# A two-layer network with routed experts in one launch: a run of one-hot products a row in the first layer's front, eight buffers for the experts' results, and the next layer's weights loaded at other places

## The chip, the core and the metric

The kernel runs on one core of one Trainium2 chip. Everything is fp32, but for the small masks and one-hots in bf16. The metric is the device time of one execution in microseconds. What can be told from no change for this kernel is about 0.5%.

A core has five engines that run side by side and meet at semaphores: TensorE (matmuls and transposes into PSUM), VectorE, ScalarE, GpSimd, and SyncE (SP), which issues most of the transfers. In the profile they are PE (PEld is its weight load), DVE, ACT, POOL and SP. Each works through its own queue in order.

## What is computed

Two layers follow each other on `x` of 4 rows x 512 tokens x 256 channels. Each normalizes, scales and shifts by a modulation, attends, adds back through a gate, and does the same around a feed-forward part.

```python
# layer 0: linear attention over each row, then routed experts
h = layernorm(x) * (1 + ca) + sa
q, k, v = split(h @ W + b)
x = x + ga * (q / |q|) * sum(k / |k| * v)          # norms and sum over the 512 tokens of a row
h = layernorm(x) * (1 + cb) + sb
logits = h @ gate_w.T                               # 32 experts in 8 groups; 3 groups kept
topk_w, topk_idx = top_k(softmax(masked), 6)
pos = cumsum(one_hot(topk_idx)) - 1                 # place of a token in its expert, over all rows
slot = expert * 48 + pos if pos < 48 else none      # 48 places an expert
y = (silu(g) * u) @ w_down[e]                       # g, u = split(x_of_slot @ w_gate_up[e])
x = x + gb * (sum_k 16 * topk_w * y[slot] + shared_expert(h))
# layer 1: 16-head causal attention, then a gated feed-forward with spline weights
```

## The kernel before

The first layer has two stages. The **front** goes through the four rows `b` one after the other (the loop `for b in range(B)` that the diff changes), and interleaves by hand, on TensorE, the pieces of several rows. The pieces are Python generators; `some(parts, n)` takes the next `n` steps of one. TensorE's instructions stay in the order in which they are written (`manual_schedule`). The other engines' queues are put in order at build by a planner, from estimated times and from the order of writing; `issue_after(ins)` keeps a block's instructions behind `ins` on the engine of `ins`. The pieces are:

- `linear_attention(b, half)`: three projections `p` (L352) of 128 channels, for values, keys and queries. ScalarE writes `vT`, squares the keys with a sum (L370), writes `qT` (L376) and squares it with a sum (L378). VectorE forms the sum over keys and values (L372). GpSimd raises the two sums to the power -1/2 (`n`, L379). VectorE then scales `kv` (L381) and forms `o` (L383).
- `attention_output(b)`: transposes `at_a` of `o` (L253), the addition to `x` (L257), the statistics, the power `rs_m` on GpSimd (L201), and the normalized `xn_m` (L213, L217).
- `attention_input(b)` and `moe_input(b)`: transposes `lt_a`, `lt_m` (L235) and the modulated copies `hT_a`, `hT_m` (L237).
- `table_rows(b)`: eight GpSimd products and sums on `xn_m` (L576, L577), and the store of the row's tokens to a table in DRAM. The gather of the experts reads this table.
- `logits(b)` and `choose(b)`: the products `plg` (L589), the transposed `plv` (L600), and on VectorE the choice of groups and experts, up to the mask `selb` (L654) and the weights `wr` (L655), with one exponential on ScalarE (L635).
- `place(b)`: the running count `pos` by matmuls (L663 to L674) and its copy `posb` (L683). For row 0 GpSimd ranks each token's experts in the steps `rk` (L688 to L696). Then, four times a row, a one-hot `oh` (128 x 1536, bf16, two buffers) on VectorE (L706) and four matmuls `pix` (L710) that turn it into slot indices, summed in `ixs` (L719).
- `shared(b)`: six products a row for the shared expert (`sg`, `su`, L736), 24 in all, taken as filler through `sh`; ScalarE and VectorE take them to `sT` (L744, L746).

In row `b`'s pass, the placing of row `b - 1` runs among the logits and the choice of row `b`: each of the four one-hots is followed by its matmuls and then by another piece. After the loop the matmuls `pid` (L805) bring the slot indices into columns, and the GpSimd gathers `xg` of the tokens (L887) start from them.

The **expert stage** goes through 16 pairs of experts. The weights `wg`, `wd` lie in eight slots: six are loaded during the front, two when the front's memory is free, and pair `q + 8` when pair `q` has freed its slot. A pair is gathered (`xg`), turned (`xt`), multiplied (`gu`, L906), turned again (`act_t`) and multiplied down (`y`, L929; one PSUM buffer). ScalarE evicts `y` to `ysb` (L943; four buffers). SP writes `ysb` to the DRAM array `ytab` (L974). For the first twelve pairs GpSimd scatters it to `planes` (L959), from which row 0's sums are read back as `yr` (L1013) when all scatters have landed. The last four pairs (`direct`) go to row 0 by a one-hot product instead (`pc`, L988); their one-hot lies in the slot of a `wd` that is no longer needed, their `ysb` in four buffers of its own (tag `ysd`). VectorE and GpSimd sum `yr` (L1029 to L1033), the row is normalized for layer 1, and layer 1's first projections `pj` start.

The loads of layer 1's first weights (`load_qk`, L846; `load_v`, L855) are written after pair 7, kept behind the last expert load.

Of the kernel before, what the change touches and what calls it, by code (L numbers as in the profile page):

```python
# [18 lines left out]
P = 128  # L19
# [17 lines left out]
SHARES = (0, 0, 0)  # L37
LAST = 1
# [47 lines left out]
def kernel(ctx: ExitStack, tc: tile.TileContext, a: dict, out: bass.AP):  # L86
# [225 lines left out]
    with ExitStack() as l0:  # L312
# [31 lines left out]
        def linear_attention(b, half, sp, ps):  # L344
# [24 lines left out]
            junk = sp.tile([P, T], F32, tag="junk", name=f"j{b}{half}", bufs=1)  # L369
            nc.scalar.activation(junk, pk, AF.Square, bias=bk, accum_out=n2[:, 0:1])  # L370
            junk2 = sp.tile([P, T], F32, tag="junk2", name=f"jj{b}{half}", bufs=1)
            nc.vector.scalar_tensor_tensor(junk2, pk, bk, vT, ALU.add, ALU.mult, accum_out=kv)  # L372
            yield
            pq = project(half)
            qT = sp.tile([P, T], F32, tag="qT", name=f"qT{b}{half}")
            nc.scalar.activation(qT, pq, AF.Identity, bias=bq[:, half : half + 1])  # L376
            junk = sp.tile([P, T], F32, tag="junk", name=f"j2{b}{half}", bufs=1)
            nc.scalar.activation(junk, qT, AF.Square, accum_out=n2[:, 1:2])  # L378
# [3 lines left out]
            o = sp.tile([P, T], F32, tag=f"o{half}", name=f"o{b}{half}", bufs=1)  # L382
# [220 lines left out]
        def choose(b, lg):  # L603
# [9 lines left out]
            gr = rp.tile([P, NTT, 16], F32, tag="gr", name=f"gr{b}")  # L613
# [28 lines left out]
            sel = rp.tile([P, NTT, E], F32, tag="sel", name=f"sel{b}")  # L642
# [15 lines left out]
        def place(b):  # L658
# [25 lines left out]
            if b:  # L684

                nc.gpsimd.memset(wr[:, :, 1, :], float(1 << 20))
            else:

                rk = [fc.tile([P, NTT, E], F32, tag=f"rk{u}", name=f"rk{u}") for u in range(2)]
                nc.gpsimd.tensor_copy(rk[0][:, :, 1:], selb[:, :, 0 : E - 1])  # L690
                nc.gpsimd.memset(rk[0][:, :, 0:1], 0.0)
                for u, w in enumerate((1, 2, 4, 8, 16)):
                    src, dst = rk[u % 2], rk[(u + 1) % 2]
                    nc.gpsimd.tensor_copy(dst[:, :, 0:w], src[:, :, 0:w])
                    nc.gpsimd.tensor_tensor(dst[:, :, w:], src[:, :, w:], src[:, :, 0 : E - w], ALU.add)
                nc.gpsimd.tensor_tensor(wr[:, :, 1, :], rk[1], six.to_broadcast([P, NTT, E]), ALU.add)  # L696
# [5 lines left out]

            pix = psa.tile([P, CAP, 8], F32, tag="lgix", name=f"pix{b}", bufs=1)
            for i in range(NTT):
                oh = rp.tile([P, CAP, E], BF16, tag="oh", name=f"oh{b}{i}", bufs=2)
                nc.vector.tensor_tensor(  # L706
                    oh, posb[:, i : i + 1, :].to_broadcast([P, CAP, E]), iota_c, ALU.is_equal
                )
                for q in range(4):
# [3 lines left out]
                        rhs=oh[:, :, 8 * q : 8 * q + 8],  # L713
# [3 lines left out]
                if i < NTT - 1:  # L717
                    yield
# [3 lines left out]
        shared_banks, last_silu = [False], [None]  # L722
# [28 lines left out]
        with tc.manual_schedule(engines={mybir.EngineType.PE}):  # L751
# [9 lines left out]
            for b in range(B):  # L761
# [4 lines left out]
                attention_output(b, sp, ps)  # L766
                some(part, 2 if more else 3)
                if more:
                    some(linear_attention(b + 1, 1, sp, ps), 4)
# [5 lines left out]
                some(placed)  # L775
# [5 lines left out]
                some(placed)  # L781
                some(sh)
                table_rows(b)
                pick = choose(b, next(lg))
                next(pick)
                some(placed)
                if not more or 0 < SHARES[b]:
                    some(sh)
                next(pick, None)
                for i in range(1, 3):  # L790
                    some(placed)
                    if not more or i < SHARES[b]:
                        some(sh)
                placed = place(b)
            some(sh, LAST)
            for n in (1, 1, 0, 0, 0):
                some(placed)
                some(sh, n)
# [4 lines left out]
        for m in range(4):  # L803
# [8 lines left out]
        with tc.manual_schedule(engines={mybir.EngineType.PE}):  # L812
            for _ in sh:
                pass
# [1104 lines left out]
```

## Time and profile before

| | us |
|---|---|
| three executions | 1154.89, 1148.79, 1153.67 |
| their median | 1153.67 |
| the profiled execution | 1150.32 |
| its span | 1148.6 |
| TensorE busy in the span | 1113.2 (97%) |
| VectorE busy | 849.7 (74%) |
| GpSimd busy | 625.5 (54%) |
| ScalarE busy | 544.1 (47%) |
| mean transfer rate over the span | 75 GB/s |

The profile is of one execution. Busy shares are averages over stages that differ: the front ends with `pid` at 131.5 us, the expert stage with layer 1's first projections at 227 us, and layer 1 takes the rest. In a timeline a row gives start, length, engine, line, operation, tile written and tiles read, and in brackets the idle time of the engine before it and what ended that. A clock of 1.0 is TensorE's full rate.

### The profile page before, as it was taken

What the parts mean: (1) busy time and instruction counts of PE and PEld (TensorE: products, weight loads), DVE (VectorE), ACT (ScalarE), POOL (GpSimd) and SP (SyncE); (2) the same over time, 40 slices, a digit from 0 to 9 for tenths busy, and PEclk for the clock granted to TensorE, in tenths of its full rate; (3) what the DMA queues carried; (4) which work ended last, traced back from release to release, by engine and by line L of the source; (5) the groups of instructions that cost most, each with busy time, mean ns of one, the idle gap of its engine ahead of it and who ended that gap; (6) DMA issues with size and microseconds to landing.
All of it is one profiled execution on the core that took longest, in us unless ns stands there. A gap on an engine that the chain in (4) does not pass through costs nothing.

```text
span 1148.6 us, 16948 instructions
## 1 busy us (share of the span) xinstructions
PE 1113.2 (97%) x5256; PEld 818.4 (71%) x5256; DVE 849.7 (74%) x2562; ACT 544.1 (47%) x1386; POOL 625.5 (54%) x944
## 2 busy tenths in 40 slices
PE   7988999999999999999999999999999999999998
PEld 3434454677777777777777777777777777888887
DVE  5669544677888878888788877988777776566765
ACT  4654233355545555555555555555555555333321
POOL 4445334368865768855756865435445655344331
PEclk9989999999999999999999999999999999999999
DMA  7830399735313223410421522111010000000000
GB/s 254 278 96 28 107 302 279 246 71 97 65 38 77 48 69 59 94 46 19 95 50 37 103 43 68 37 50 39 22 44 19 28 11 1 1 1 19 19 5 33
DMA packets 80486, 86.10 MB, mean 75 GB/s; under 512 B 12158, under 2 KB 64748, under 8 KB 80268
## 3 DMA queue, kind: packets, MB, share of 16 engines
q1 hardware_dynamic: 67868, 70.19, 19.6%
q0 software_dynamic: 11712, 13.25, 7.2%
q10 hardware_dynamic: 816, 1.58, 0.4%
q8 instruction: 42, 0.69, 0.3%
q14 instruction: 48, 0.39, 0.1%
HBM read 73.84 MB, written 11.55 MB: 74 GB/s over the span
## 4 chain that ended last, share of the span: by engine, by line
PE 74%; DVE 9%; ACT 3%; DMA 2%; issue 2%; POOL 1%; ACTq 0%; POOLq 0%; DVEq 0%; SPq 0%
PE s L1410 11%; PE o L1451 10%; PE po L1147 8%; PE P0p L1147 7%; PE fP L1147 6%; PE pt L1442 6%; PE P1p L1147 4%; PE P2p L1147 4%; PE P0v L1147 3%; PE acc L1147 3%; PE P2v L1147 2%; PE P1v L1147 2%; PE pd L823 2%; PE gu L906 1%; PE y L929 1%
## 5 line engine op out<-in xcount | busy, mean ns | idle before, releaser
L1425 ACT ACTIVATE p<-s,nm 128x512 f32<-128x512 f32 (+3 forms) x256 | 135.4, 529 | 119.9 <-DVE nm L1422 119.1
L1410 PE MATMUL s<-qk,qk 128*128 128x512 f32 (+3 forms) x512 | 170.4, 435 | 1.5 <-DVE qk L1318 1.4
L1451 PE MATMUL o<-pT,v 128*128 128x512 f32 (+3 forms) x512 | 148.5, 433 | 0.0
L1451 PEld LDWEIGHTS o<-pT,v 128*128 128x128 f32 x512 | 96.7, 190 | 54.7 <-issue 30.6
L1444 ACT COPY pT<-pt 128x512 f32<-128x512 f32 (+1 forms) x192 | 98.4, 513 | 67.1 <-PE pt L1442 66.9
L1422 DVE TENSOR_REDUCE nm<-s 128x1 f32<-128x512 f32 (+3 forms) x256 | 124.3, 485 | 4.0
L290 POOL DMA_INDIRECT ysum<-ytab,code x72 | 112.9, 1568 | 20.4 <-issue 14.8
L1427 DVE TENSOR_SCALAR p<-p,den 128x512 f32<-128x512 f32 (+3 forms) x256 | 118.1, 461 | 3.4
L1442 PEld LDWEIGHTS pt<-ident,p 128*128 128x128 f32 x640 | 81.6, 141 | 34.5 <-issue 10.5
L1442 PE MATMUL pt<-ident,p 128*128 128x128 f32 x640 | 101.7, 273 | 0.4 <-DVE p L1427 0.4
L1420 DVE TENSOR_TENSOR s<-s,mask 128x128 f32<-128x128 f32 x256 | 73.7, 288 | 30.1 <-PE s L1410 30.0
L1285 POOL TENSOR_TENSOR w_p<-w_q,w_k 128x128 f32<-128x128 f32 x63 | 39.2, 622 | 82.4 <-ACT t1p L1324 55.0
L1410 PEld LDWEIGHTS s<-qk,qk 128*128 128x128 f32 x512 | 77.4, 191 | 6.5 <-issue 1.9
L1147 PE MATMUL P0p<-hT_a,w_q 128*128 128x256 f32 x252 | 75.0, 379 | 0.0
L1293 POOL TENSOR_TENSOR w_p<-w_k 128x128 f32<-128x128 f32 x63 | 29.9, 474 | 80.4 <-PE P2p L1147 80.4
L1147 PEld LDWEIGHTS P0p<-hT_a,w_q 128*128 128x128 f32 x252 | 47.5, 190 | 33.1 <-issue 30.1
L1426 DVE RECIPROCAL den<-den 128x1 f32<-128x1 f32 x256 | 40.5, 158 | 37.9 <-ACT p L1425 35.4
L1147 PE MATMUL P1p<-fT,w_p 128*128 128x256 f32 x252 | 64.9, 380 | 1.1 <-DVE x L257 1.1
L1462 ACT ACTIVATE oH<-o,bia 128x512 f32<-128x512 f32 x64 | 43.9, 686 | 42.4 <-PE o L1451 41.6
L1155 POOL TENSOR_TENSOR fI<-it 128x256 f32<-128x256 f32 x30 | 21.8, 726 | 67.1 <-DVE it L1744 67.1
L1318 DVE SCALAR_TENSOR_TENSOR qk<-P0p,bia,u3p 128x256 f32<-128x256 f32 x63 | 30.4, 483 | 36.7 <-ACT qk L1339 36.0
L1147 PEld LDWEIGHTS P1p<-fT,w_p 128*128 128x128 f32 x252 | 47.6, 190 | 8.4 <-issue 2.1
(336 smaller groups left out, 2666.1 us busy)
## 6 DMA issues: line engine op xcount, KB each, us to landing
wg<-in_w_gate_up SPq DMA_DIRECT2D x16, 704.0 KB
w_q<-in_w_q SPq DMA_DIRECT2D x64, 128.0 KB
w_k<-in_w_k SPq DMA_DIRECT2D x64, 128.0 KB
w_v<-in_w_v SPq DMA_DIRECT2D x16, 512.0 KB
wd<-in_w_down SPq DMA_DIRECT2D x16, 352.0 KB
basis<-in_basis SPq DMA_DIRECT2D x8, 640.0 KB
planes<-zero SPq DMA_DIRECT2D x4, 768.0 KB
yr<-planes SPq DMA_DIRECT2D x4, 768.0 KB
```

The costliest lines, as they stand in the source:

```text
L290: ga = nc.gpsimd.indirect_dma_start(out=ysum[b][:, i, :], out_offset=None, in_=ytab[:, :], in_offset=bass.IndirectOffsetOnAxis(ap=code[:, ...
L1147: nc.tensor.matmul(out, lhsT=lhsT, rhs=rhs, start=start, stop=stop, skip_group_check=shared)
L1410: nc.tensor.matmul(s[:, at[i] : c], lhsT=qk[n, 0][:, i * P : (i + 1) * P], rhs=qk[n, 1][:, : (i + 1) * P], start=True, stop=True,)
L1420: nc.vector.tensor_tensor(s[:, e - P : e], s[:, e - P : e], mask, ALU.add)
L1422: nc.vector.tensor_reduce(nm, s[:, e - w : e], AX.X, ALU.max, negate=True)
L1425: nc.scalar.activation(p, s[:, e - w : e], AF.Exp, bias=nm, accum_out=den)
L1426: nc.vector.reciprocal(den, den)
L1427: nc.vector.tensor_scalar_mul(p, p, den)
L1442: nc.tensor.transpose(pt[:, c : c + P], probs[n, i][:, j * P : (j + 1) * P], ident)
L1444: nc.scalar.copy(pT, pt[:, :w])
L1451: nc.tensor.matmul(o[:, j * P :], lhsT=vs[n // 4][:, j, hc : hc + HD], rhs=pTs[n, j], start=(j == 0), stop=(j == NTT - 1),)
L1462: nc.scalar.activation(oT, o, AF.Identity, bias=bia[:, 2, h : h + 1])
```

## The change

Four things change.

1. In the front, the four one-hots of a row are made in one run, in four buffers instead of two, and the sixteen `pix` matmuls follow in one run later. The last step of the second half of `linear_attention` (`kv`, `o`) is written behind the one-hots and kept there with `issue_after(last_oh)`. The rank steps `rk` of row 0 are kept behind the last power written on GpSimd.
2. The table products of row `b - 1` are written into the pass of row `b`, behind `attention_output(b)`. The fillers of the shared expert are dealt out anew: 2, 4, 4 and 11 products in the four passes (2, 3, 3 and 10 before), two more behind the loop (3 before, with `LAST`), and one behind `pid` (3 before). `pid` is now in the written order on TensorE.
3. `ysb` has eight buffers. The `ysb` of the last four pairs lies with their one-hot in the freed `wd` slot. Memory for the new buffers comes from `junk` and `junk2`, whose results go to `qT`, `vT` and `o`, and from `gr` and `sel`, which get one buffer.
4. `load_qk(0)`, `load_v(0)` and `load_qk(1)` are written in the passes of pairs 9, 10 and 11, without the tie to the last expert load, and `load_qk(2)` behind the read-back.

```diff
             bk = bq[:, 2 + half : 3 + half]
-            junk = sp.tile([P, T], F32, tag="junk", name=f"j{b}{half}", bufs=1)
-            nc.scalar.activation(junk, pk, AF.Square, bias=bk, accum_out=n2[:, 0:1])
-            junk2 = sp.tile([P, T], F32, tag="junk2", name=f"jj{b}{half}", bufs=1)
-            nc.vector.scalar_tensor_tensor(junk2, pk, bk, vT, ALU.add, ALU.mult, accum_out=kv)
+
+            qT = sp.tile([P, T], F32, tag="qT", name=f"qT{b}{half}")
+            nc.scalar.activation(qT, pk, AF.Square, bias=bk, accum_out=n2[:, 0:1])
+            nc.vector.scalar_tensor_tensor(vT, pk, bk, vT, ALU.add, ALU.mult, accum_out=kv)
             yield
             pq = project(half)
-            qT = sp.tile([P, T], F32, tag="qT", name=f"qT{b}{half}")
             nc.scalar.activation(qT, pq, AF.Identity, bias=bq[:, half : half + 1])
-            junk = sp.tile([P, T], F32, tag="junk", name=f"j2{b}{half}", bufs=1)
-            nc.scalar.activation(junk, qT, AF.Square, accum_out=n2[:, 1:2])
+            o = sp.tile([P, T], F32, tag=f"o{half}", name=f"o{b}{half}", bufs=1)
+            nc.scalar.activation(o, qT, AF.Square, accum_out=n2[:, 1:2])
             last_pow[0] = nc.gpsimd.tensor_tensor(n2, n2, nhalf[:, 0:2], ALU.pow)
...
                 rk = [fc.tile([P, NTT, E], F32, tag=f"rk{u}", name=f"rk{u}") for u in range(2)]
-                nc.gpsimd.tensor_copy(rk[0][:, :, 1:], selb[:, :, 0 : E - 1])
...
+                with tc.issue_after(last_pow[0].ins):
+                    nc.gpsimd.tensor_copy(rk[0][:, :, 1:], selb[:, :, 0 : E - 1])
...
+            ohs = []
+            for i in range(NTT):
+                oh = rp.tile([P, CAP, E], BF16, tag="oh", name=f"oh{b}{i}", bufs=NTT)
+                last_oh[0] = nc.vector.tensor_tensor(
+                    oh, posb[:, i : i + 1, :].to_broadcast([P, CAP, E]), iota_c, ALU.is_equal
+                )
+                ohs.append(oh)
+            yield
             pix = psa.tile([P, CAP, 8], F32, tag="lgix", name=f"pix{b}", bufs=1)
             for i in range(NTT):
-                oh = rp.tile([P, CAP, E], BF16, tag="oh", name=f"oh{b}{i}", bufs=2)
-                nc.vector.tensor_tensor(
-                    oh, posb[:, i : i + 1, :].to_broadcast([P, CAP, E]), iota_c, ALU.is_equal
-                )
                 for q in range(4):
                     nc.tensor.matmul(
                         pix[32 * q : 32 * q + 32, :, :],
                         lhsT=tok[:, b * NTT + i, :],
-                        rhs=oh[:, :, 8 * q : 8 * q + 8],
+                        rhs=ohs[i][:, :, 8 * q : 8 * q + 8],
                         start=(i == 0),
                         stop=(i == NTT - 1),
                     )
-                if i < NTT - 1:
-                    yield
...
                 attention_output(b, sp, ps)
+                if b:
+                    table_rows(b - 1)
                 some(part, 2 if more else 3)
                 if more:
-                    some(linear_attention(b + 1, 1, sp, ps), 4)
+                    part = linear_attention(b + 1, 1, sp, ps)
+                    some(part, 3)
...
                 moe_input(b, sp, ps)
-                some(placed)
+                some(placed, 2)
+                if more:
+                    with tc.issue_after(last_oh[0].ins) if b else nullcontext():
+                        some(part)
                 some(sh)
...
                 lg = logits(b, ps)
                 next(lg)
-                some(placed)
                 some(sh)
-                table_rows(b)
                 pick = choose(b, next(lg))
                 next(pick)
-                some(placed)
-                if not more or 0 < SHARES[b]:
+                if not more:
+                    some(placed)
+                if b:
                     some(sh)
+                if more:
+                    some(placed)
                 next(pick, None)
-                for i in range(1, 3):
-                    some(placed)
-                    if not more or i < SHARES[b]:
-                        some(sh)
+                if not more:
+                    some(sh, 3)
                 placed = place(b)
-            some(sh, LAST)
-            for n in (1, 1, 0, 0, 0):
-                some(placed)
-                some(sh, n)
+            table_rows(B - 1)
+            some(placed, 2)
+            some(sh, 2)
+            some(placed)
...
-                ysb = xp.tile(
-                    [P, D], F32, tag=("ysb", "ysd")[direct], name=f"ysb{q}", bufs=4
-                )
+                if direct:
+
+                    both = freed("wd", q - 2, [P, D + T], f"both{q}")
+                    ysb, oh = both[:, :D], both[:, D:]
+                else:
+                    ysb = xp.tile([P, D], F32, tag="ysb", name=f"ysb{q}", bufs=8)
...
                     back.append(yr)
+                load_qk(2)
                 with tc.issue_after(rd.ins):
                     load_v(1)
...
-                    if q == NPAIR - NLOAD:
-                        with tc.issue_after(last_load[0].ins):
-                            load_qk(0)
-                            load_v(0)
-                            for n in (1, 2):
-                                load_qk(n)
+                    if NPAIR - NLOAD < q < NPAIR - NDIR:
+
+                        (lambda: load_qk(0), lambda: load_v(0), lambda: load_qk(1))[q - NPAIR + NLOAD - 1]()
```

## The prediction

> **What bounds the kernel now.** I read the page first, then the windows of 25 us, then the timelines of each engine up to 232 us.
>
> ```profile
> span 1148.6 us, 16948 instructions
> ...
> PE 1113.2 (97%) x5256; PEld 818.4 (71%) x5256; DVE 849.7 (74%) x2562; ACT 544.1 (47%) x1386; POOL 625.5 (54%) x944
> ...
> PEclk9989999999999999999999999999999999999999
> ```
>
> TensorE is busy for 97% of the span, so only its idle time and its half-rate time can be won. Past 300 us it is idle for 1 to 2 us in 100, and the change touches nothing there. What is left lies in the front (up to the slot matmuls `pid` at 131.5 us) and the expert stage (to 227 us). In the TensorE timeline (start, length, line, tile, count, and in brackets the idle time ahead with its releaser) the front's waits are:
>
> ```profile
> 68.32 0.35 PE L710 MATMUL pix<-oh,tok 128*32 128x384 bf16 x4 [2.78 <-DVE oh L706]
> ...
> 73.17 0.51 PE L710 MATMUL pix<-oh,tok 128*32 128x384 bf16 x4 [0.87 <-DVE oh L706]
> 73.61 5.10 PE L352 MATMUL p<-hT_a,W 128*128 128x512 f32 x8
> ...
> 93.08 0.35 PE L710 MATMUL pix<-oh,tok 128*32 128x384 bf16 x4 [1.07 <-DVE oh L706]
> ...
> 97.96 0.35 PE L710 MATMUL pix<-oh,tok 128*32 128x384 bf16 x4 [1.74 <-DVE oh L706]
> ```
>
> Most wait for the one-hots `oh`, and after the 2.78 us gap eight projections take 5.10 us where the same eight take 3.60 at 47.60. VectorE's timeline says why `oh` is late:
>
> ```profile
> 65.48 0.27 DVE L381 TENSOR_SCALAR kv<-kv,n 128x1 f32<-128x1 f32 x1 [3.70 <-POOL n L379]
> 65.79 0.99 DVE L383 TENSOR_SCALAR o<-qT,kv,mod 128x512 f32<-128x512 f32 x1
> ...
> 67.01 2.56 DVE L706 TENSOR_TENSOR oh<-posb,iota_c 128x1536 bf16<-128x1536 bf16 x2
> ```
>
> ```profile
> 89.03 0.85 DVE L655 SCALAR_TENSOR_TENSOR wr<-wr,selb 128x128 f32<-128x128 f32 x1
> ...
> 90.59 1.03 DVE L383 TENSOR_SCALAR o<-qT,kv,mod 128x512 f32<-128x512 f32 x1
> ...
> 125.12 1.83 DVE L706 TENSOR_TENSOR oh<-posb,iota_c 128x1536 bf16<-128x1536 bf16 x2
> ```
>
> VectorE is held for 3.70 us by `kv`, which needs the power `n` from GpSimd, and the `oh` are queued behind `kv`. GpSimd has `n` behind the ten rank steps `rk` (61.53 to 64.74):
>
> ```profile
> 55.35 0.71 POOL L379 TENSOR_TENSOR n<-n,nhalf 128x2 f32<-128x2 f32 x1 [6.78 <-ACT j L378]
> 56.03 1.01 POOL L201 TENSOR_TENSOR rs_m<-rs_m,nhalf 128x4 f32<-128x4 f32 x1
> ...
> 64.74 0.71 POOL L379 TENSOR_TENSOR n<-n,nhalf 128x2 f32<-128x2 f32 x1
> ```
>
> Two `oh` take 2.56 us while GpSimd multiplies table rows, 1.83 without (125.12). In the expert stage the evictions `ysb` wait for a buffer whose write to `ytab` has not landed, and TensorE waits for the eviction:
>
> ```profile
> 171.16 0.95 ACT L943 ACTIVATE ysb<-y,xg 64x256 f32<-64x256 f32 x2 [4.57 <-DMA ytab<-ysb]
> ...
> 197.28 0.95 ACT L943 ACTIVATE ysb<-y,xg 64x256 f32<-64x256 f32 x2 [3.23 <-DMA ytab<-ysb]
> ```
>
> ```profile
> 172.16 1.97 PE L929 MATMUL y<-wd,actT 88*64 88x256 f32 x8 [2.39 <-ACT ysb L943]
> 173.92 2.11 PE L906 MATMUL gu<-wg,xT 128*64 128x352 f32 x8
> ...
> 199.33 2.61 PE L906 MATMUL gu<-wg,xT 128*64 128x352 f32 x8
> ```
>
> There are four buffers, and a write that was issued is waited for until 8 to 14 us later (issue at 157.24, eviction at 171.16), behind weights in the same queue. The transfers themselves are nearly full (columns: TensorE, weight load, VectorE, ScalarE, GpSimd busy; clock; DMA share; GB/s):
>
> ```profile
> 150.00:175.00 25.00, 22.61 (x143) 12.08 (x144) 14.30 (x63) 9.03 (x22) 12.34 (x12) 0.94 0.99 303
> 175.00:200.00 25.00, 22.79 (x142) 10.32 (x140) 10.12 (x45) 8.40 (x21) 9.62 (x11) 0.98 0.94 278
> ```
>
> **The change part by part.** No engine instruction is added or removed but for positions; `junk` and `junk2` only change their destination, on engines that run in order, and the single-buffer `gr` and `sel` are touched by VectorE alone: cost 0, bounded by one sub-0.2 us wait a row either way.
>
> *Row 1 (the iteration that turns row 1 and places row 0).* `kv` and `o` go behind the `oh`, `rk` behind `n`: the 3.70 us hold goes. Against it, the eight GpSimd products of the row before (5.86 us alone, 42.66 to 48.37; 8.1 beside VectorE, 89.01 to 97.15) now follow `rs_m` (57.04), beside two `xn`, `wr`, `o`, `sc`, `sel`, `dp`, `wr`. The rows that show such a meeting: `wr` 0.85 against 0.29 (61.49), `o` 1.03 against 0.53. [...] I take 2.2, ends 0 and 5.6. `selb` then comes at 61.46 + 2.2 = 63.7, and `pos` 1.2 us later than 62.45. Then `posb` ends at 64.3, four `oh` at 0.94 end at 68.1, `kv` and `o` at 68.9, the eviction `sT` at 69.5. TensorE does two shared products (1.75 each) and the logits (0.6) until 68.1; the third, new here, waits for the bank until 69.5, ends at 71.3, the sixteen `pix` matmuls (1.1) at 72.4. Before: 73.6, one product less, then 1.5 us lost to the clock.
>
> *Row 2.* From 72.4, TensorE reaches `pos` in 15.5 - 1.5 = 14.0 us, at 86.4; but `selb` follows the transposes `at_a` (3.6 us in) by 10.45 us before, 12.65 now: 88.7. With the same 9.1 us as in row 1 (`pos` 0.4 longer) the row ends at 97.8. Before: 98.2. So 0.4 us and two products (3.5 us) are ahead.
>
> *Row 3 and the tail.* Here VectorE is the bound: busy from 98 to 124 us but for 1.8 us. It starts 1.0 us sooner, loses about 1.4 to rows 2 and 3 of the table both running on GpSimd, and has four `oh` at 1.2 us ahead of `gs`, which comes 0.9 us later; but the last `oh`, `ixs` and one `sT` (2.0 us) no longer lie between `gs` and `selb`, so `selb` is 1.1 us sooner. After it the `oh` run takes 3.75 us where 125.12 to 130.05 took 4.9, so `pid` starts near 129.4, **2.1 us sooner**. One shared product instead of two is left behind `pid`; the gather (7.3 us from `pid`'s end to the second `xt`) is covered for 4.4 us, so about 2.9 us of idle instead of 0.84: no cost of its own, for the gather is the path, but the clock may fall after it (priced below).
>
> *Eight `ysb`, direct results in the freed `wd`.* `ysb` 8 to 11 then reuse buffers written over 25 us before: all waits go. TensorE: 2.39 + 0.76 + 1.45 = 4.6 idle, and half-rate: `y` 1.97 for 1.08 and `gu` 2.11 for 1.40 (1.6), `gu` 2.61 for 1.40 and the next two (1.55): 7.75 us. [...] I keep 7.75, and 4.6 for the low end. On the path to the last scatter lie 2.39 + 1.6 + 0.76 and the 2.4 us that `ysb` 11 waits (197.28, where `y` ended at 194.84): **7.2 us**.
>
> *What is late next: the transfers.* The read-back `yr` is issued at 202.84, when the last scatter has landed, behind the weights. Idle share between 150 and 204 us is 25 x 0.01 + 25 x 0.06 and 0.8 after 200: 2.6 us. `w_q`, `w_k` of head 2 (256 KB at 0.29 MB/us: 0.9 us) go behind `yr`. The stage's loads start when the last shared product has freed its memory: 136.1 before, 129.4 + 1.1 + 1.75 = 132.2 now, 3.9 sooner. So transfers allow 2.6 + 0.9 + 3.9 = 7.4 us, TensorE 2.1 + 7.2 = 9.3; the smaller counts. The 1.9 us of difference also swallows a half-rate spell (1.6) behind the gather. The other next-layer loads move from one group at 186 to 197 us into pairs 9 to 11 without a tie to the last expert load: if they go out between expert loads, 1.0 MB is 3.5 us of delay to weights that have some 3 us of slack; near 0 by their rows (186.26 to 196.93), so 0, with 0 to 3.5 as bounds. `scale_q` of head 2 (218.46) needs the moved load; `yr` plus 256 KB end some 11 us after 195.4, 4 us ahead of it; if not, ScalarE's copies behind it wait. SP has only `ytab` stores and `win` behind those loads, for which nobody waits before 243.
>
> From 209 us on, `yr`'s sums, the norm and the first head follow as before. **Sum: 7.4 us.** The profiled execution took 1150.32 us (span 1148.6); its 7.4 less is 1142.9. The runs' median is 1153.67; the four executions average 1151.9, so I forecast 1144.5 (0.5% is 5.8 us, what a measurement of this kernel tells from none).
>
> **The rivals.** *Both gains in full* (chance 0.15): row clashes cost nothing and the loads keep pace; front 4 to 6, experts 7.75: about 1139. For: 2.6 us of idle transfer time may be more once waits go; against: the 0.99 share.
> *Transfers or VectorE eat it* (0.24): clashes cost the rule's 5.6 a row, the front gives 0, the stage only 2.6 + 0.9: 1148.5. For: `selb` had 0.1 us of slack in row 2, and the DMA share.
> *Slower: GpSimd starts the moved table products ahead of the power `n` of the next row's first half* (0.15). At 55.35 and 56.03 `n` went 0.7 us ahead of `rs_m`; if that order turns, `n` waits 5.9 to 8 us, `kv` with it, and the norm and choice behind `kv`; `pos` loses 6 us in each of two rows, with a half-rate spell (2 to 3.6) each: 16 us, against 10 us of front stalls removed and 5 of the stage, where those do not shrink. With `oh` late too the old stalls stay: +12 - 5: 1159. It decides as soon as one of the eight precedes `n`; the order of GpSimd and VectorE is set at build, and the diff does not show it.
>
> **How the numbers follow.** The forecast has 0.46: 4 to 11 us less, above the bound in four fifths of it. Faster: 0.37 + 0.15 = 0.52. Same: 0.09 + 0.19 = 0.28. Slower: 0.15 + 0.05 from the second rival's bad end = 0.20. Range 1136 to 1157: the full gain below, most of the slower case's approach above, with 3 us of spread between executions; the forecast's own range is 1141 to 1149.
>
> **What would show it.** Right: no 3.70 us before `kv` at 65; `oh` in runs of four near 0.94; no wait of `ysb` for `ytab`; clock 1.0 at 70 to 76 and 172 to 175; `pid` near 129, first `yr` work near 201. Wrong: `pos` waiting over 3 us for `selb`, `n` behind table products, `gu` waiting for `wg`, or `yr` still issued after 200.

## The result, and the profile after

| | before | after |
|---|---|---|
| median of 20 runs each, us | 1152.86 | 1155.30 |
| lowest and highest, us | 1147.90, 1155.53 | 1151.53, 1159.72 |
| span of the profiled execution, us | 1148.6 | 1153.1 |

The ratio is 1.0036, with a 95% interval of 1.0024 to 1.0048: some 4 us slower, where 7.4 less were forecast. That is inside the half per cent that was called no change, though the interval lies wholly above 1. From the page of after:

```profile
PE 1113.4 (97%) x5256; PEld 818.8 (71%) x5256; DVE 854.6 (74%) x2562; ACT 544.5 (47%) x1386; POOL 623.8 (54%) x944
```

TensorE has the same work (1113.4 us for 1113.2); what moved is idle and half-rate time before 232 us. Two lengths tell it, read from TensorE's timeline of one profiled execution each: **F**, from row 0's `plv` (47.49 in before, which the change leaves alone) to the start of `pid`, and **S**, from there to layer 1's first `pj` (227.32). Measuring from `plv` takes out what differs at the start: in after the first eight projections took 5.87 us where before took 4.40, same order, same inputs, and 1.65 us are gone before any piece that the change puts elsewhere. F is 84.0 in before and 84.4 in after, S 95.8 and 97.5. The forecast wanted F 2.1 shorter and S about 5 shorter. But F varies with the execution. Five profiles show before's front: 84.0 in before, 81.8 in e1, e6 and e14 below, 85.3 in e5; the two long ones hold a spell at half clock (0.50 from 70 to 76 us in before) that the three short ones do not. After's front has 84.4 or 84.5 in four profiles (after, e2, e3, e9). Against the short ones after loses 2.7 us in F.

TensorE in after, front and gather:

```profile
67.13 0.22 PE L659 MATMUL pos<-selb,tri 128*128 128x128 bf16 x1 [2.45 <-DVE selb L650]
...
112.47 0.22 PE L659 MATMUL pos<-selb,tri 128*128 128x128 bf16 x1 [3.72 <-DVE selb L650]
...
133.57 1.13 PE L810 MATMUL pid<-two,ixs 128*64 128x4 f32 x16
...
139.33 0.47 PE L901 MATMUL xt<-ident,xg 128*128 128x128 f32 x2 [0.33 <-issue]
144.27 0.70 PE L901 MATMUL xt<-ident,xg 128*128 128x128 f32 x2 [4.46 <-DMA xg<-table,idx]
```

The gaps of 2.78 and 1.74 us ahead of `pix` are gone, as forecast. In their place `pos` waits for `selb` 2.45 us in row 1 and 3.72 in row 3, the forecast's own sign of failure. `pid` stands at 133.57. Then the second `xt` waits 4.46 us for its gather; before had 0.84. The windows there (columns as in the prediction) show the half clock behind that gap:

```profile
140.00:144.00 4.00, 0.00 (x0) 0.00 (x0) 0.32 (x1) 0.00 (x0) 3.08 (x4) 1.00 0.92 313
144.00:148.00 4.00, 3.32 (x8) 2.16 (x8) 0.42 (x1) 0.79 (x3) 1.49 (x5) 0.54 1.02 355
148.00:150.00 2.00, 2.00 (x7) 0.77 (x8) 0.00 (x0) 0.37 (x1) 0.00 (x0) 0.50 1.01 284
150.00:152.00 2.00, 2.00 (x9) 1.12 (x6) 0.34 (x1) 0.32 (x1) 0.00 (x0) 0.71 1.00 283
```

In the expert stage the eight buffers do what was forecast: no eviction waits for `ytab`, and no `y` waits for an eviction (2.39, 0.76 and 1.45 us in before). TensorE makes up 6.3 of the 8.0 us by which the second `gu` is late (152.45 for 144.48; last `y` at 210.38 for 208.67).

Yet `pj` comes 3.7 us late. The last scatter is issued at 201.14 (198.51 in before), which is 67.6 us behind `pid` for 67.0: what the buffers gave, the gap behind the first gather had taken. The read-back `yr` follows at 205.86 (202.84 in before). SyncE's queue in front of it:

```profile
200.44 0.37 SPq L850 DMA_DIRECT2D w_q<-in_w_q  x1
200.85 0.47 SPq L850 DMA_DIRECT2D w_k<-in_w_k  x1
201.36 3.37 SPq L1655 DMA_DIRECT2D win<-in_windows  x3
...
205.86 2.07 SPq L1019 DMA_DIRECT2D yr<-planes  x4
```

### The profile page after: what moved, and what is told of

Read it like the earlier page. It is cut to its first block, busy times and chain, and to the rows that moved or that the text cites. A ratio compares the mean times of both kernels' runs of the same rounds, so it can differ in the third digit from the quotient of the medians.

```text
span 1153.1 us, 16941 instructions
## 1 busy us (share of the span) xinstructions
PE 1113.4 (97%) x5256; PEld 818.8 (71%) x5256; DVE 854.6 (74%) x2562; ACT 544.5 (47%) x1386; POOL 623.8 (54%) x944
## 4 chain that ended last, share of the span: by engine, by line
PE 79%; DVE 11%; ACT 3%; POOL 2%; issue 2%; DMA 2%; SPq 0%; ACTq 0%; POOLq 0%; DVEq 0%
PE s L1414 11%; PE o L1455 10%; PE po L1151 8%; PE P0p L1151 7%; PE fP L1151 6%; PE pt L1446 6%; PE P1p L1151 4%; PE P2p L1151 4%; PE P0v L1151 3%; PE acc L1151 3%; PE p L350 2%; PE P2v L1151 2%; PE P1v L1151 2%; PE gu L910 2%; PE y L933 1%
## 5 line engine op out<-in xcount | busy, mean ns | idle before, releaser
L1448 ACT COPY pT<-pt 128x512 f32<-128x512 f32 (+1 forms) x192 | 98.4, 513 | 67.6 <-PE pt L1446 65.6
```

What stands on the lines that cost most here:

```text
L1448: nc.scalar.copy(pT, pt[:, :w])
```

## The experiments

All ratios are to the kernel before, with 95% intervals. F and S are from each run's one profile.

| run | edit | ratio | F | S |
|---|---|---|---|---|
| before | | 1 | 84.0 | 95.8 |
| after | | 1.0036 [1.0024, 1.0048] | 84.4 | 97.5 |
| e1 | before + eight `ysb` | 1.0007 [0.9991, 1.0022] | 81.8 | 98.2 |
| e2 | before + front | 1.0019 [1.0004, 1.0034] | 84.5 | 98.2 |
| e3 | after, `sc` cleared first | 1.0019 [1.0007, 1.0030] | 84.4 | 97.6 |
| e4 | after, table at old place | 0.9968 [0.9954, 0.9983] | 79.2 | 97.9 |
| e5 | before + `yr` first | 0.9987 [0.9976, 0.9999] | 85.3 | 96.4 |
| e6 | e1 + `yr` first | 0.9959 [0.9942, 0.9975] | 81.8 | 91.5 |
| e7 | e4 + `yr` first | 0.9938 [0.9922, 0.9954] | 79.2 | 93.3 |
| e8 | e4, three products behind `pid` | 0.9990 [0.9976, 1.0005] | 79.2 | 99.6 |
| e9 | after + `yr` first | 0.9987 [0.9978, 0.9996] | 84.4 | 93.6 |
| e10 | e8 + `yr` first | 0.9934 [0.9920, 0.9948] | 79.1 | 94.8 |
| e11 | after, row 2's table at old place | 1.0015 [1.0002, 1.0028] | 84.9 | 95.7 |
| e12 | before + `rk` behind the power | 0.9937 [0.9922, 0.9951] | 78.3 | 96.7 |
| e13 | e12 + table moved | 1.0065 [1.0041, 1.0089] | 90.0 | 97.6 |
| e14 | e1 + `win` behind `yr` | 0.9987 [0.9971, 1.0003] | 81.8 | 91.8 |
| e15 | e6 + e12 | 0.9922 [0.9901, 0.9943] | 78.3 | 91.8 |

### The parts of the change: e1, e2, e3, e4

e1 takes the `ysb` edit alone into before; e2 is after without that edit and without the new places of the loads. The new places of the loads were not run by themselves.

```diff
-                ysb = xp.tile([P, D], F32, tag=("ysb", "ysd")[direct], name=f"ysb{q}", bufs=4)
+                if direct:
+                    both = freed("wd", q - 2, [P, D + T], f"both{q}")
+                    ysb, oh = both[:, :D], both[:, D:]
+                else:
+                    ysb = xp.tile([P, D], F32, tag="ysb", name=f"ysb{q}", bufs=8)
```

> The kernel before, with the eight ysb buffers and the direct results in the freed wd slots alone; front and loads as before. Theory (the stage's gain is real but the read-back of row 0 follows the transfers): the waits of ysb for ytab go, TensorE runs 5 to 7 us ahead of before by pair 11, the first yr is issued 1 to 3 us sooner than at 202.84, time 1 to 3 us less (1150 to 1152 for 1153). Rival 1 (TensorE bounds the stage): 6 to 7 us less (about 1146). Rival 2 (loads pushed earlier crowd something out): no change or slower.

Rival 2 came in: no change. TensorE gained (its last `y` stands 71.1 us behind `pid`, 77.2 in before), the last scatter was issued at 191.64 instead of 198.51 (61.5 us behind `pid` for 67.0), and `yr` all the same at 200.96 (70.8 behind `pid` for 71.3). SyncE's queue of e1:

```profile
193.39 0.37 SPq L846 DMA_DIRECT2D w_q<-in_w_q  x1
195.26 0.37 SPq L846 DMA_DIRECT2D w_k<-in_w_k  x1
195.73 2.64 SPq L976 DMA_DIRECT2D ytab<-ysb  x4
198.42 2.31 SPq L1653 DMA_DIRECT2D win<-in_windows  x3
200.96 2.08 SPq L1015 DMA_DIRECT2D yr<-planes  x4
```

> The kernel after without the ysb part and without the written places of the next layer's loads, so the new front on the old expert stage. Theory (the new front is a loss: pos waits for selb behind the table products, and the gather lies uncovered): pid 2 us later than before, second xt 4 us later, time 3 to 6 us more than before. Rival (the front is neutral, and the loss lies in the loads between the expert loads): within 2 us of before.

The new front alone is 0.2% slower, less than expected, and its interval overlaps that of after.

> The kernel after with one move: GpSimd clears the tile sc of the next modulation ahead of the seven gathers, not behind them. Theory A (ScalarE stands 12.4 us before the silu into sc, with the copies of pd behind it, and this costs TensorE the gap of 4.46 us at 139.7 and the half clock after it): the gap shrinks to under 1 us, the second xt comes up to 4 us sooner, the time is 1 to 4 us less than after. Theory B (the second xt waits for its gather, which comes then anyway): the second xt still comes 9 to 10 us behind the end of pid, the time is that of after (1.003 to 1.004 of before).

```diff
-            for q in range(7):
-                fetched(q)
...
-            with tc.issue_after(last_silu[0].ins):
-                w1, s1 = load_mod_inputs(m1p, 1, nc.scalar)
...
+            with tc.issue_after(last_silu[0].ins):
+                w1, s1 = load_mod_inputs(m1p, 1, nc.scalar)
+            with tc.issue_after(cleared[0].ins):       # the memset of sc
+                for q in range(7):
+                    fetched(q)
```

The copies of `pd` went ahead of the second `xt`, and it still came at 146.09. The clearing had to wait for the last reader of the memory under `sc` (`su`, 136.87), and held the gathers back by 2.0 us with it. ScalarE's wait was not what the gap came from; the gather was. The time can't be told from after's.

> The kernel after with the table products back in their old place (row b's behind its logits), all else as after, the order on VectorE and TensorE too. Theory (the moved products hold VectorE in both its norms and choices): xn_m back to 0.7 us from 1.63, wr, sel, sc and dp near their short forms, pos waits under 1.5 us for selb in row 3 (3.72 in after), pid 3 to 5 us sooner than in after, time 2 to 4 us less than after, so at or below before. Rival (the four one-hots ahead of gs hold row 3, not the table): pos still waits over 3 us, no change against after. Second rival: the oh runs then meet the table products (1.3 us each), and the gain is under 1 us.

```diff
-                if b:
-                    table_rows(b - 1)
...
+                table_rows(b)
                 pick = choose(b, next(lg))
...
-            table_rows(B - 1)
```

Only GpSimd's order differs from after. F falls by 5.2 us and the time from 1.0036 to 0.9968 of before: the table products were the front's loss. `pos` waits 0.62 us in row 3. The gap at the second `xt` (4.04 us) and S (97.9) stay.

### What held the read-back: e5, e6, e7, e9, e14

The cut shows e5 and e6; in e7 and e9 `load_qk(1)` leaves pair 11 and `load_qk(2)` its place before `rd`, to the same end.

```diff
-                            for n in (1, 2):
-                                load_qk(n)
...
                 with tc.issue_after(rd.ins):           # rd: the last load of yr
+                    load_qk(1)
                     load_v(1)
+                    load_qk(2)
...
+              with tc.issue_after(rd.ins):
                 for j in range(3):
                     nc.sync.dma_start(out=win[...], ...)
```

> The kernel before with one change of order on SyncE: the loads of heads 1 and 2 and the three win loads stand behind the read-back yr, no longer ahead of it. Theory (in before the last scatter, 198.51, and its landing set the read-back; the queue ahead of it costs little): yr issued at 201 to 203, time within 1.5 us of before. Rival (the loads and the slow small packets of win hold yr in any case): yr issued by 200, 2 to 4 us less.

> The kernel before with the eight ysb buffers and with that order on SyncE. In e1 the last scatter came 6.9 us sooner than in before and yr only 1.9, since ytab, the next heads' loads and win lie ahead of yr in SyncE's queue. Theory (that queue took the stage's gain): yr issued at 196 to 199, layer 1's first projections 2 to 4 us sooner than in e1 (228.4), time 2 to 4 us less than before. Rival 1 (the transfers as a whole bound the row's sums, whatever their order): yr lands at 205 to 207 all the same, no change. Rival 2 (TensorE's or VectorE's work behind yr takes over): yr 3 us sooner, projections under 1 us sooner.

> The kernel of e4 (after with the table products in their old place) with yr ahead of the loads of heads 1 and 2 and of win. Theory (e4 is held by SyncE's queue: last scatter 194.57, yr 199.39): yr at 197 to 198, time 1 to 3 us less than e4 (0.997 of before), so about 0.994 to 0.996 of before. Rival (the transfers bound it whatever the order): as e4.

> The kernel after with yr ahead of the loads of heads 1 and 2 and of win on SyncE, as in e7, the table products where after has them. Theory (the loss of after is the table products at 2 us before pid and the gather, and SyncE's queue held the stage's gain): pid as in after (133.6), yr issued 1 to 3 us behind the time of the last scatter's landing at 204 to 205, time 1 to 3 us less than after: 1.000 to 1.002 of before. Rival (with the front late, the queue has no part in it): 1.0036 as after.

With four `ysb` the order matters little (e5: S 96.4, 0.13% less time). With eight S is shorter by 6.7 us (e1 to e6), 4.5 (e4 to e7) and 3.9 (after to e9), and the time by 0.3 to 0.5%. e9, which is after with this one order, is 0.13% faster than before. SyncE in e6:

```profile
190.22 4.95 SPq L976 DMA_DIRECT2D ytab<-ysb  x4
195.79 1.99 SPq L1015 DMA_DIRECT2D yr<-planes  x4
197.84 0.64 SPq L846 DMA_DIRECT2D w_q<-in_w_q  x1
```

So the eight buffers' gain was real, and was waiting in SyncE's queue: in e1 the last `ytab` stores, `win` and head 2's two loads stood between the last scatter and `yr`, which went 9.3 us after it; in e6 `yr` goes 6.5 us after it.

Not all of these differences in S are the queue's. In e1, e4 and after two evictions of `y` (pairs 3 and 5) came late, and the last scatter stands 1.7, 2.6 and 1.9 us further behind `pid` than in e6, e7 and e9. That is ahead of the loads that were moved, and e8 and e11 below, whose SyncE order is that of e4 and after, do not have it; its cause stays open. The pair that is free of it is e8 and e10 (below): there the last scatter stands 62.9 us behind `pid` in both, and the order alone brings `yr` forward by 3.6 us behind `pid`, S by 4.7 and the time by 0.6%. e8 (`pid` at 127.17):

```profile
190.09 1.02 POOL L961 DMA_INDIRECT planes<-ysb,didx  x1 [1.75 <-ACT ysb L946]
200.29 1.91 SPq L1015 DMA_DIRECT2D yr<-planes  x4
```

and e10 (`pid` at 127.59):

```profile
190.50 1.02 POOL L961 DMA_INDIRECT planes<-ysb,didx  x1 [1.76 <-ACT ysb L946]
197.12 2.06 SPq L1015 DMA_DIRECT2D yr<-planes  x4
```

e7 is after with the old table place and `yr` first. Its 0.9938 is some 7 us below before, near the 7.4 that was forecast for the whole change. That the sizes agree so well is in part luck: its S is only 2.5 us below that of before, where some 5 were wanted.

e14 takes only the last of these three edits, on e1.

> The kernel of e1 (before with the eight ysb buffers) with the three win loads behind yr, the heads' loads still ahead of it. Theory A (the small packets of win hold yr: their issue took 2.31 us in e1, while the transfers moved under 100 GB/s): yr issued near 198.4, most of e6's gain: 0.996 to 0.998 of before. Theory B (the heads' loads, 768 KB at about 0.27 MB/us, are what is ahead): yr near 200, 0.999 to 1.001.

The profile says A (S 91.8), the times say neither: 0.9987 lies between. The profiled execution (1144.21) is the fastest of that kernel (the slowest took 1153.96), so its S is the better end. How much of e6's gain is `win` stays open.

### The gather: e8, e10

```diff
-            some(placed, 2)
-            some(sh, 2)
-            some(placed)
+            some(placed, 3)
```

> The kernel of e4 with the last three products of the shared expert behind pid, as in before, instead of one. Theory (pid is set by VectorE's chain selb, posb, oh, and the hole of 4 us between the first two xt with its half clock is lack of cover): pid within 0.5 us of e4 (127.0), the hole under 1 us, no half clock behind it, gu of pair 1 up to 4 us sooner than 146.0; the time 1 to 3 us less than e4 unless the transfers hold the end. Rival (the gathers come late because the loads start right behind them): memory comes free later and with it the loads, gathers land sooner, and the later loads cost the stage what the cover gives: as e4 or worse.

> The kernel of e8 (table products in their old place, three products behind pid) with yr ahead of the later loads. In e8 gu of pair 1 came 2.8 us sooner than in e4, but yr 0.9 later. Theory (there too SyncE's queue ate it): last scatter near 190, yr issued at 196 to 197, time 1 to 3 us below e7 (0.9938 of before): 0.991 to 0.993. Rival (the loads, which start 5 us later than in e4, bound it): as e7 or worse.

With three products behind `pid` the gap is gone and the second `gu` is 2.8 us sooner than in e4, but the time is not less (0.9990 for 0.9968, intervals that overlap): the rival. The first loads of the stage start when the last product is done: `wg` of pair 6 is issued 10.2 us behind `pid`, 4.9 in e4. With `yr` first the two are alike (e10 0.9934, e7 0.9938): e10's last scatter goes 2.0 us sooner behind `pid` than e7's, and its `yr` does not (69.5, 69.3). Cover costs loads and loads cost cover; neither deal of the products is better.

### Where the table products hurt: e11, e12, e13

```diff
-                if b:
+                if b in (1, 2):
                     table_rows(b - 1)
...
+                if b == 2:
+                    table_rows(2)
                 pick = choose(b, next(lg))
```

> The kernel after with row 2's table products alone back in their old place, so that row 3's pass has only its own products on GpSimd; rows 0 and 1 stay where after has them. Theory (row 3 is where the move costs most, since two rows of products meet its norm, its choice and its four one-hots): pos of row 3 waits under 1.5 us for selb, pid 3 to 5 us sooner than in after, time 2 to 4 us less than after: about before. Rival (row 1's 2.45 us count as much): pid 1 to 2 us sooner only, time 1.001 to 1.003 of before.

The theory fell. `pos` of row 3 waits only 0.61 us, yet it stands where it stood, since the products of row 2 then meet its four one-hots:

```profile
90.55 5.16 DVE L703 TENSOR_TENSOR oh<-posb,iota_c 128x1536 bf16<-128x1536 bf16 x4
...
96.54 2.69 PE L735 MATMUL su<-hT_m,wsgu 128*128 128x512 f32 x4 [2.41 <-DVE sT L745]
...
112.12 0.22 PE L659 MATMUL pos<-selb,tri 128*128 128x128 bf16 x1 [0.61 <-DVE selb L650]
```

Four `oh` take 5.16 us (3.56 without GpSimd), `su` waits 2.41 us for `sT`, and the clock is halved from within `su` on (0.92 in 96 to 98 us, 0.50 in 98 to 100, 0.73 in 100 to 102). Moving a row's products moves the cost.

> The kernel before with the rank steps rk of row 0 kept behind the power n on GpSimd, nothing else. Theory (the 3.70 us hold of kv was real and lay on the path to pid, the rest of the front's change is not needed for it): no hold of kv at 65, the 2.78 us wait of pix gone and its half clock, row 1 ends 2 to 4 us sooner, pid 1 to 3 us sooner, time 1 to 3 us less than before unless the transfers take it. Rival (rows 2 and 3, bound by VectorE, swallow it): pid within 0.5 us, no change.

```diff
+                with tc.issue_after(last_pow[0].ins):
-                nc.gpsimd.tensor_copy(rk[0][:, :, 1:], selb[:, :, 0 : E - 1])
+                    nc.gpsimd.tensor_copy(rk[0][:, :, 1:], selb[:, :, 0 : E - 1])
...
```

This is the one piece of the change's front that pays: F 78.3, the time 0.6% less, more than was expected. (That is 7 us in five executions, interval 6 to 9; F shows 3.5 to 7.0 of it, by which profile of before's front it is set against.) The run of four one-hots, the new deal of the products and the old table place (e4, F 79.2) do not improve on it.

> The kernel of e12 (before with rk behind the power) with one more edit: the table products of row b - 1 stand in row b's pass behind the power of its norm, as in after. Only GpSimd's order differs from e12. Theory (the table move alone makes the front late): xn_m near 1.6 us in rows 1 and 3, pos waits 2 us or more for selb in one of these rows, pid 4 to 6 us later than in e12 (126.1), time 3 to 6 us more than e12, so 0.997 to 0.999 of before. Rival (the move hurts only together with the run of four one-hots and the dealt fillers): pid within 1.5 us of e12, time 0.994 to 0.995 of before.

```diff
                 attention_output(b, sp, ps)
+                if b:
+                    table_rows(b - 1)
...
-                table_rows(b)
                 pick = choose(b, next(lg))
...
+            table_rows(B - 1)
             some(sh, LAST)
```

e13 differs from e12 in GpSimd's order alone, so it prices the move. VectorE in row 1 (with rows left out), first e12:

```profile
57.34 0.16 DVE L208 SCALAR_TENSOR_TENSOR nmr_m<-ag_m,rs_m 128x4 f32<-128x4 f32 x1 [0.70 <-POOL rs_m L201]
57.42 0.73 DVE L217 TENSOR_SCALAR xn_m<-x,ag_m,rs_m 128x256 f32<-128x256 f32 x2
58.07 0.28 DVE L639 TENSOR_TENSOR wr<-wr,ssum 128x128 f32<-128x128 f32 x1
58.27 0.54 DVE L383 TENSOR_SCALAR o<-qT,kv,mod 128x512 f32<-128x512 f32 x1
...
58.93 0.22 DVE L644 TENSOR_SCALAR sel<-wr 128x128 f32<-128x128 f32 x1
...
61.51 0.26 DVE L654 TENSOR_SCALAR selb<-dr 128x128 bf16<-128x128 f32 x1
```

and e13:

```profile
57.50 0.68 DVE L208 SCALAR_TENSOR_TENSOR nmr_m<-ag_m,rs_m 128x4 f32<-128x4 f32 x1 [0.70 <-POOL rs_m L201]
58.10 1.63 DVE L217 TENSOR_SCALAR xn_m<-x,ag_m,rs_m 128x256 f32<-128x256 f32 x2
59.65 0.82 DVE L639 TENSOR_TENSOR wr<-wr,ssum 128x128 f32<-128x128 f32 x1
60.39 0.94 DVE L383 TENSOR_SCALAR o<-qT,kv,mod 128x512 f32<-128x512 f32 x1
...
61.99 0.74 DVE L644 TENSOR_SCALAR sel<-wr 128x128 f32<-128x128 f32 x1
...
65.51 0.23 DVE L654 TENSOR_SCALAR selb<-dr 128x128 bf16<-128x128 f32 x1
```

while GpSimd did its eight products in 5.9 us, nearly as fast as alone (added up 6.01 us, 5.86 in before; here the first and last pair of them):

```profile
57.44 1.41 POOL L576 TENSOR_TENSOR xn_m<-xn_m,rows 128x256 f32<-128x256 f32 x2
...
61.89 1.45 POOL L577 TENSOR_TENSOR xn_m<-xn_m,rows 128x256 f32<-128x256 f32 x2
```

Eight VectorE instructions in a row are each 0.4 to 0.5 us longer (`xn_m` is two: 0.73 becomes 1.63; `sc` and `dp` go from 0.29 to 0.81 and 0.71), `selb` comes 3.8 us later behind the start of `nmr_m`, and `pos` waits 2.59, 3.62 and 3.83 us for it in the three rows. F grows by 11.7 us, the time by 1.3%. The move hurts by itself. In after it costs less (5.2 us of F against e4), and there `pos` waits in two rows, not three; which of the other edits spares the third was not tried.

### The gains together: e15

> The kernel before with three edits: rk behind the power (e12), eight ysb, and yr ahead of the later loads (both e6). Theory (the gains add: 0.9937 and 0.9959): pid near 126, yr issued near 191 to 193, time 0.988 to 0.991 of before (1138 to 1142). Rival (with the front earlier the loads of experts fall behind and bound the stage): 0.992 to 0.994, as e12 or e10.

F and S have both gains in full, and the ratio is the lowest of all, but its interval overlaps those of e7, e10 and e12. In time the two would give 0.990 (0.9937 times 0.9959), just under the interval; six executions do not settle whether they add. The rival's sign is there, the last `gu` waits for its weights,

```profile
189.97 2.61 PE L907 MATMUL gu<-wg,xT 128*64 128x352 f32 x8 [2.09 <-DMA wg<-in_w_gate_up]
```

as one does for 1.79 us in e6, and in before none does there; S shows no loss from it. e15 beats before by 0.8% (median 1142.3 us in its runs), and after by more.

## Why the prediction was wrong

**The 3.70 us hold: right, and undersized.** `kv` no longer waits, and e12 shows that `rk` behind the power is worth 3.5 us of F against three of the five profiles of before's front, and 5.7 and 7.0 against the two with a spell at half clock.

**Clashes on VectorE: the step that failed.** The term was 2.2 us a row between ends of 0 and 5.6, an estimate of mine: about half of the eight VectorE instructions for 0.5 us each, at the upper end all eight for the 0.7 us of a GpSimd product. No run shows 2.2, nor the 5.6 a row of the second rival. From `nmr_m` to `selb` in row 1 it is 3.8 (e13 against e12: 8.0 for 4.2) and 3.9 in after against before. e4, where the move alone is undone, shows that it made the whole of the front's loss: 5.2 us of F and 0.7% of the time. The rows that I took, `wr` and `o`, had the size right, about 0.5 us each. That only half would meet was a guess, and wrong: VectorE's chain and the eight products start from the same `rs_m` and run beside each other for all of it, and in e13 each of eight VectorE instructions there is 0.4 to 0.5 us longer. The upper end's count of eight was right (with `nmr_m` in the place of the last `wr`), its 0.7 us for each too much. `MAX8` (0.47 for four) and `MATCH_REPLACE8` (0.18) kept their length, in e13 as in e12.

**Row 3: undersized for the same reason.** I gave 1.4 us to two rows of products. `nmr`, `xn_m`, `sc`, `sel`, `dp` and `selb` of row 3 are all long there, and the four `oh` behind them take 5.18 us; `pos` waits 3.72 us. That put `pid` behind, not 2.1 us ahead.

**The half clock as a fixed price: wrong.** I credited 1.5 us in row 1 to the end of a half-rate spell. e1 has the same gap and no spell:

```profile
69.23 0.35 PE L710 MATMUL pix<-oh,tok 128*32 128x384 bf16 x4 [2.78 <-DVE oh L706]
...
73.69 3.70 PE L352 MATMUL p<-hT_a,W 128*128 128x512 f32 x8
```

The projections behind a gap of 2.78 us took 3.70 us there and in e6 and e14, but 5.10 in before and 5.01 in e5. What can be won is the gap; the spell comes in some executions. Of the 7.75 us forecast for the expert stage 3.15 are of this kind. In before's windows of 2 us the clock is 0.51 (172 to 174) behind the gap of 2.39 us and 0.50 (200 to 202) behind 1.45, but 1.00 (98 to 100) behind 1.74.

**The gather: "no cost of its own" was wrong.** I took before's 7.3 us as given, and 2.9 of idle. It is 9.6 in after (134.7 to 144.27), the idle time is 4.8, and the spell behind it, priced at 1.6, costs 3.4 (my estimate from the windows above: 6.8 us at half clock). The second `gu` stands 18.9 us behind `pid`, 13.0 in before. e8 shows that the missing cover is the products behind `pid`. They did not only fill time, they also held back transfers. In before two gathers left ahead of the 1.5 MB of `wmod`:

```profile
133.17 1.25 POOL L887 DMA_INDIRECT xg<-table,idx  x1 [12.82 <-DVE idxf L816]
...
134.72 0.97 POOL L887 DMA_INDIRECT xg<-table,idx  x1 [0.30 <-issue]
...
135.18 1.01 ACTq L137 DMA_DIRECT2D wmod<-in_wmod  x2
```

and in after one:

```profile
135.82 1.25 POOL L891 DMA_INDIRECT xg<-table,idx  x1 [16.47 <-DVE idxf L820]
...
136.74 0.42 ACTq L130 DMA_DIRECT2D cT<-in_cT  x1
...
137.20 1.01 ACTq L135 DMA_DIRECT2D wmod<-in_wmod  x2
137.37 0.97 POOL L891 DMA_INDIRECT xg<-table,idx  x1 [0.30 <-issue]
```

With the last silu out of the way early, `wmod` starts right behind the first gather and the first `wg` behind the second (4.9 us behind `pid`, 7.5 in before). That it is these loads which lengthen the second gather is a reading of the queues; no run held `wmod` alone back.

**Eight `ysb`: right.** 7.2 us were forecast on the path to the last scatter. Behind `pid` it is issued 5.5 us sooner in e1 (with the two late evictions), 7.3 in e6 and 7.2 in e14. The last `y` of e1 gains 6.0.

**The transfers as a bound: the other step that failed.** I added their idle share (2.6 us), head 2's loads (0.9) and an earlier start (3.9) to 7.4 and took that for what could be won. With `pid` late the first `wg` started only 0.5 us sooner (138.47 for 139.01). And I put head 2's loads behind `yr` because they are written there. They stand ahead of it in SyncE's queue (200.44, 200.85 in after), and `win` with them, which I had named only as harmless to others. The sum had no term for the order of this one queue, and the order decided: with the same bytes, `yr` was issued 69.5 us behind `pid` in e10 and 73.1 in e8, 66.2 in e6 and 70.8 in e1. In after it is worth 0.5% of the time (e9).

**Loads between expert loads: not separable.** `w_q` and `w_k` of head 0 did go out at 154.31 and 157.58, between expert loads. e2, which keeps them at 190.87, can't be told from after; but two of its `win` loads went out at 153.72 and 156.99, so it is no clean test.

Of the rivals, "transfers or VectorE eat it" named both causes but held each for a limit on the gain, not for a loss. In the slower rival the products went ahead of the power `n`; GpSimd kept `n` of the first half ahead (57.12 for `n`, 58.76 for the first product in after, and the same order in e13), so it was the clashes, not a held `kv`, that made the kernel slower.

## What to carry to other kernels

When work of one engine is moved beside another's, ask first whether both chains start from the same event: if they do, count every instruction of the kinds that the trace shows to clash, not half of them, and take the price of one from its rows. Before a stall is counted as won, read the queue ahead of the next transfer on the path, in the order in which it stands and not as it is written. And test the smallest edit of a bundle by itself: here one condition on the order gave all of the front's gain, and the rest of the bundle spent it. A stage length of one profile is a sample: the same front measured 81.8 to 85.3 us.

## What the runs showed of the hardware

The same idle gap on TensorE, 2.78 or 2.79 us at the same place, was followed by the half clock in two profiles of five (before, e5). A gap of 2.44 to 2.46 us ahead of `pos` in row 1 kept the full clock in after, e2, e3 and e9 and lost it in e11; 2.24 (e4, row 2) kept it, 2.41 (e11) and 2.39 (before) lost it. The spells came in three lengths. Added up from the granted clock in windows of 1 us (a window at 0.75 counts as half of it at half clock), those between 40 and 232 us lasted 3.4, 6.8 or 10.2 us and nothing between, 29 spells in 17 profiles: 3.4 in before at 172 us, 6.8 at 69, 6.8 in after at 144, 10.2 in e5 at 68. By that a spell takes 1.7, 3.4 or 5.1 us of TensorE's work, if TensorE is busy through it (my estimate, half of each length). So gaps of 2.4 to 2.8 us were followed by the half clock in some executions and not in others; what decides it, no run shows.

VectorE does not always pay alone. In row 1 of e13 GpSimd's eight products nearly kept their length (added up 6.01 us, 5.86 alone in before). Beside the run of four `oh` both were held: in row 3 of after `oh` took 5.18 us for 3.56 (128.61 in after, no GpSimd product beside it), and two products 2.84 where two took 1.4 to 1.6 in e13:

```profile
113.59 5.18 DVE L703 TENSOR_TENSOR oh<-posb,iota_c 128x1536 bf16<-128x1536 bf16 x4
```

```profile
113.71 2.84 POOL L572 TENSOR_TENSOR xn_m<-xn_m,rows 128x256 f32<-128x256 f32 x2
```

Three `win` loads of 24 KB each took SyncE 2.3 us to issue in e1, while the transfer engines were about 0.8 busy at 0.36 to 0.57 of the rate that `yr` then reached (e1, share and GB/s last). Which of the transfers then under way kept the rate low was not separated:

```profile
196.00:200.00 4.00, 4.00 (x20) 1.85 (x17) 1.22 (x4) 1.41 (x4) 0.00 (x0) 1.00 0.78 227
200.00:204.00 4.00, 4.00 (x16) 1.67 (x15) 0.00 (x0) 1.40 (x3) 0.00 (x0) 1.00 0.86 146
204.00:208.00 4.00, 4.00 (x15) 2.65 (x14) 0.00 (x0) 1.70 (x3) 0.92 (x1) 1.00 0.96 401
```
